# A 3x3 convolution in two transformed directions: patches of 4 rows x 2 columns for images 1 to 3, with their input sums in the order of the work

## The chip, the cores and the metric

One core of a Trainium2 chip runs the whole kernel. Its engines work side by side, each through its own queue in program order: PE multiplies matrices (with a path for loading weights, PEld), DVE (VectorE) and ACT (ScalarE) read and write SBUF and PSUM, POOL (GpSimd) works on SBUF, and SP issues DMAs. [...] The metric is the device time of the program in microseconds.

## What is computed

The input is x, four images of 256 channels, 48 x 48 pixels, f32. Two layers with a residual each:

- Layer 0: group norm of x, a 3x3 convolution 256 to 256 channels, batch norm with given statistics, relu; then q, k and v by a 256 to 768 product, attention over the 2304 pixels in 8 heads of 32, and a projection; the result is added to x.
- Layer 1: group norm; a 3x3 convolution to 45 channels gives, after a softmax over groups of nine, the weights of five dynamic 3x3 filters with dilations 1, 6, 12, 24 and 36; the input and the five filtered copies go through a 1x1 product (1536 to 256), then a batch norm over all images; the result is added.

The change concerns the 3x3 convolution of layer 0:

```
x = lax.conv_general_dilated(Vx, conv_w, window_strides=(1, 1), padding='SAME', ...)
x = x + conv_b[None, :, None, None]
inv = bn_gamma * lax.rsqrt(bn_var + BN_EPS)
x = x * inv[None, :, None, None] + (bn_beta - bn_mean * inv)[None, :, None, None]
x = jax.nn.relu(x)
```

## The kernel before

Channels lie on the 128 partitions in two halves (NH = 2). The loop over images (from `u_next = None` near L1792 on) has three kinds of stages. Image 0 first gets its convolution and q, k, v alone. Then, for each image b, comes its attention (`attention`, L978), which fills PE, DVE and ACT; and after it a mixed stage: the dynamic filters of image b (`dynamic_filters`, L1139) together with the convolution and q, k, v of image b + 1 (`conv_qkv`, L913). The last mixed stage, b = 3, has no convolution.

**The convolution.** `conv` (L765) works on patches of 4 output rows. An input of six rows is turned into six sums v[0] to v[5] (`inputs`, L773), each product i of the six multiplies its sum by its own transformed weights u[i], and `outputs` (L821) turns the six products back into four rows. Only the row direction is transformed: each product still runs over the three columns kx of the kernel. The image is split into two halves g of six patches each, so one matmul has 6 x 48 = 288 columns; a product has 2 g x 2 output groups o x 2 input halves h x 3 kx = 24 matmuls, an image 144. One PSUM buffer takes six matmuls (one product, g, o), and there are two such buffers (`ps_c`, L1797). The products come in `ORDER` = 1, 2, 3, 4, 0, 5. For image 0 DVE makes the input sums; for images 1 to 3 POOL does, on 600 elements at a time, all of them at the beginning of the convolution (`when`, L868 on). DVE and ACT empty PSUM: products 1 and 3 are copied by ACT, 2 and 4 become a sum and a difference with them on DVE, and 0 and 5 finish the rows, which ACT then scales, shifts and rectifies into `hid`.

**The weights.** `Made` (L728) makes u[i] from the convolution weights during image 0 and stores each to DRAM as `u_d[i]` (768 KB). For images 1 to 3 `taken` (L722) fetches them again, one product ahead, into a pool of two buffers; the same pool lends the attention its scratch and the last stage four homes.

**The order of the work.** The program is written out by hand (`manual_schedule`). A small planner, `Clock` (L687), holds a time for PE, DVE, ACT and POOL, advanced by a price per operation. In a mixed stage `drive` (L1625) holds several streams (weights' loads, far filters, near filters, the softmax of the filter weights, the 1x1 mix), each of which says from when it could go on; the first that is due by PE's time goes on, and if none is, one step of `other`, the convolution, is emitted; if that is used up, PE's time jumps. The near filter works in taps: ACT copies a weight row into PSUM (wb, L1448), DVE multiplies (prod, L1461), POOL adds (near, L1466). Before `drive`, the stage emits some convolution by `run(2400)` and `run(2500)` (L1653, L1667), between the steps of the group norm. What no stream left room for is emitted after it (`run(1e9)`), followed by q, k and v.

Fetches of u, of filter weights (ws) and stores stand in one queue, SP's. The two padded images (`pads`) alternate: one holds the image whose filters run, the other the normalized input of the convolution; both are loaded again from x at the start of an attention (`load_pad`, L1950).

Of the kernel before, what the change touches and what calls it, by code (L numbers as in the profile page):

```python
# [16 lines left out]
N = HH * WW  # L17
# [40 lines left out]
def conv_preact_kernel(  # L58
# [483 lines left out]
    u_d = tc.dram_tile([6, P, NH, 3, C], F32, name="u_d")  # L542
# [3 lines left out]
    with tc.tile_pool(name="w", bufs=1) as wpool, tc.tile_pool(  # L546
        name="act", bufs=1
    ) as act, tc.tile_pool(name="u", bufs=2) as upool, tc.manual_schedule():
# [12 lines left out]
        wqkv = wpool.tile([P, NH, 3, C], F32, tag="wqkv", name="wqkv")  # L561
        wp = wpool.tile([P, NH, C], F32, tag="wp", name="wp")
# [53 lines left out]
        bn_s6 = wpool.tile([P, NH], F32, tag="bn_s6", name="bn_s6")  # L616


        pads = []
        for j in range(2):  # L620
            t = act.tile([P, NH, PADW * PADW], F32, tag=f"pad{j}", name=f"pad{j}")
            t = t.rearrange("p h (r w) -> p h r w", w=PADW)
            nc.gpsimd.memset(t[:, :, 0, :], 0.0)
            nc.gpsimd.memset(t[:, :, PADW - 1, :], 0.0)
            nc.gpsimd.memset(t[:, :, 1 : PADW - 1, 0], 0.0)
            nc.gpsimd.memset(t[:, :, 1 : PADW - 1, PADW - 1], 0.0)
            pads.append(t)

# [58 lines left out]
        class Clock:  # L687
# [11 lines left out]
            def level(self):  # L699
                self.t = dict.fromkeys(self.t, max(self.t.values()))  # L700
# [21 lines left out]
        def taken(i):  # L722

            u = upool.tile([P, NH, 3, C], F32, tag="u", name=f"u_{i}")
            nc.sync.dma_start(out=u, in_=u_d[i])
            return u

        class Made:  # L728


            def __init__(self, wc, pool):
                self.w = [wc[:, :, 3 * j : 3 * j + 3, :] for j in range(3)]
                self.u = {}
                self.pool = pool

# [9 lines left out]

            def home(self, i):
                return upool.tile([P, NH, 3, C], F32, tag="u", name=f"u_{i}")
# [4 lines left out]
            def __call__(self, i):  # L752
# [9 lines left out]
                nc.sync.dma_start(out=u_d[i], in_=u[i])  # L762
                return u[i]

        def conv(b, gn, psum_tile, weights, ready, pool, hid, between):  # L765
# [115 lines left out]
            for at, i in enumerate(ORDER):  # L881
                u = ahead
                for g in range(2):
# [5 lines left out]
                    if g == 0 and at + 1 < len(ORDER):  # L889
                        ahead = weights(ORDER[at + 1])  # L890
                    for o in range(NH):
# [20 lines left out]

        def conv_qkv(b, gn, psum_tile, weights, ready, pool, between=()):  # L913

            hid = keep("h", f"hid_{b}")
            yield from conv(b, gn, psum_tile, weights, ready, pool, hid, between)
# [6 lines left out]
            for c in range(NCK):  # L923
                cols = slice(c * CH, (c + 1) * CH)
                for g in range(NH):
                    for s, dst, bias in ((0, q, Q_B), (1, k_, K_B)):
# [18 lines left out]
                        )  # L945
                        yield 2 * MM
# [31 lines left out]
        def attention(b, q, k_, vT, pools, spare, project, scratch):  # L978
# [132 lines left out]
            weigh(*steps[-1], prev)  # L1111
            close(last)
            return ao, chunk
# [25 lines left out]
        def dynamic_filters(b, ao, chunk, norm, other, pools):  # L1139
# [153 lines left out]
            def far():  # L1293

                for c in range(NCK):
# [6 lines left out]
                    held[0] = True  # L1302
                    for h in range(NH):
                        at = moved(
# [6 lines left out]
                        )  # L1311
# [313 lines left out]
            def drive(streams):  # L1625

                due = [next(s, None) for s in streams]
                while any(d is not None for d in due):
# [9 lines left out]
                    else:  # L1638
                        got = next(other, None)
                        if got is not None:  # L1640
                            spent[0] += got
                        elif soonest < NEVER:
                            clock.t["PE"] = soonest

            if alone:
                other = late()


            while chunk < NCK:
# [23 lines left out]
            if alone:  # L1673
                streams = [last_back(), *streams, last_loads()]
            drive(streams)
# [116 lines left out]
        u_next = None  # L1792
        norms = {}
        for b in range(B + 1):

            with tc.tile_pool(name=f"work1_{b}", bufs=2) as work1, tc.tile_pool(
# [13 lines left out]
                if b < B:  # L1810
                    weights, between = taken, ()
                    if b == 0:
# [62 lines left out]
                if b == 0:  # L1875
                    for j, _ in enumerate(other):
                        if j == 0:
# [5 lines left out]
                            nc.vector.tensor_scalar(bn_s6, bn_s, -1.0 / 6.0, None, ALU.mult)  # L1883
                            table(AF.Exp)
# [8 lines left out]
                else:  # L1893
                    if b == B:
# [15 lines left out]
                        for j in range(2):  # L1910
                            t = upool.tile([P, NH, 3, C], F32, tag="u", name=f"yu_{j}")
                            t = t.rearrange("p h k c -> p (h k c)")
# [150 lines left out]
```

## Time and profile before

| | |
|---|---|
| runs of the program | 2769.19, 2769.86, 2770.11 us; median 2769.86 |
| the profiled execution | 2766.55 us |
| its span, first to last instruction | 2764.8 us |
| PE, DVE, ACT, POOL busy | 2638.8, 2025.3, 1761.1, 632.3 us |
| mean granted PE clock | 0.99 |
| convolution and q, k, v of image 0 | to about 147 us |
| mixed stages | about 516 to 818, 1190 to 1492, 1861 to 2136 us |
| last stage | from about 2510 us |

Lines of the profile begin with the line of the program, the engine and the operation, then output <- inputs, the shape (partitions x elements) and xcount; after the bars come busy us and the mean of one in ns, then the idle time just before, with what ended it. In lines of the order of work the first number is the start in us and the second the length, and square brackets hold the idle time before it. In tables by stage each engine has its busy us and number of records; the last three columns are PE's clock, the share of the DMA engines, and GB/s. An f32 matmul leaves two records, and its own length is longer than the step to the next, since matmuls overlap.

### The profile page before, as it was taken

The page shows a single profiled execution, that of the slowest core. Times are in us where ns is not written, and L with a number is a line of the kernel's source. Part 1 is how long each engine was busy: PE and PEld are TensorE (multiplying, and loading weights), DVE is VectorE, ACT ScalarE, POOL GpSimd, SP SyncE. Part 2 cuts the span into 40 slices and gives each one's busy share as a digit, 9 for nine tenths or more (in the row PEclk, how much of TensorE's full clock was granted, in tenths as well). Part 3 has the DMA queues.
Part 4 walks back from the last instruction along what each step waited for, and adds up shares of the span by engine and source line. Part 5 has one row for each costly group of instructions (what it writes and reads, how often), then busy time and mean ns, then how long its engine had stood idle before and what let it go on. Part 6 is the DMA issues. An engine that isn't in the chain of part 4 may idle for free. (4 is left out here: it accounts for less than half of the span.)

```text
span 2764.8 us, 42248 instructions
## 1 busy us (share of the span) xinstructions
PE 2638.8 (95%) x17108; PEld 1135.8 (41%) x17108; DVE 2025.3 (73%) x1956; ACT 1761.1 (64%) x2153; POOL 632.3 (23%) x583
## 2 busy tenths in 40 slices
PE   7999999899999999989999999999999999999994
PEld 5632223455662222345565222245566222234452
DVE  6578888656539888856644988894664988885476
ACT  3488988633349888843336889882335988873244
POOL 5100100435400100054430001006542001000352
PEclk9999999999999999999999999999999999999997
DMA  5604544223422444423360345442335244432465
GB/s 216 156 24 103 109 98 104 58 77 90 104 56 58 101 102 97 109 57 75 84 132 9 81 98 112 101 87 56 93 92 150 55 96 95 101 87 68 118 181 182
DMA packets 132522, 267.35 MB, mean 97 GB/s; under 512 B 55656, under 2 KB 97552, under 8 KB 131424
## 3 DMA queue, kind: packets, MB, share of 16 engines
q0 software_dynamic: 25952, 135.74, 21.6%
q1 hardware_dynamic: 106368, 128.84, 17.7%
q8 instruction: 136, 2.23, 0.3%
q14 instruction: 66, 0.54, 0.1%
HBM read 107.40 MB, written 34.46 MB: 51 GB/s over the span
## 5 line engine op out<-in xcount | busy, mean ns | idle before, releaser
L1050 DVE TENSOR_TENSOR acc<-acc,p 128x2048 f32<-128x2048 f32 (+1 forms) x572 | 1061.1, 1855 | 115.6 <-ACT p L1014 64.9
L1014 ACT ACTIVATE p<-se 128x1536 f32<-128x1536 f32 x648 | 938.7, 1449 | 0.1
L1005 PE MATMUL so<-q,k 32*128 32x512 f32 (+1 forms) x1440 | 726.4, 592 | 13.5 <-ACT p L1013 12.7
L1005 PE MATMUL se<-q,k 32*128 32x512 f32 (+1 forms) x4320 | 735.1, 592 | 0.0
L1034 PE MATMUL num<-p,vT 128*32 128x512 f32 (+1 forms) x5760 | 705.1, 560 | 4.6 <-ACT p L1014 2.4
L1013 ACT ACTIVATE p<-so 128x512 f32<-128x512 f32 x648 | 388.4, 599 | 186.8 <-PE se L1005 80.0
L1466 POOL TENSOR_TENSOR near<-near,prod 128x768 f32<-128x768 f32 x192 | 348.8, 1817 | 431.4 <-DVE prod L1461 424.7
L1005 PEld LDWEIGHTS so<-q,k 32*128 32x128 f32 x1440 | 216.1, 183 | 529.0 <-ACT p L1013 489.8
L1034 PEld LDWEIGHTS num<-p,vT 128*32 128x32 f32 x5760 | 133.8, 108 | 478.8 <-issue 444.3
L1054 POOL DMA_DIRECT2D scratch<-p x124 | 105.5, 851 | 772.3 <-ACT p L1014 519.8
L1461 DVE TENSOR_TENSOR prod<-wb,pad 128x768 f32<-128x768 f32 x192 | 181.9, 953 | 87.6 <-ACT wb L1448 75.6
L1561 PE MATMUL py<-far,wsc 128*128 128x384 f32 x704 | 236.7, 488 | 0.0
L1005 PEld LDWEIGHTS se<-q,k 32*128 32x128 f32 x4320 | 226.7, 183 | 5.4 <-ACT p L1014 4.1
L1448 ACT COPY wb<-ws 128x384 f32<-128x384 f32 x216 | 108.7, 507 | 171.3 <-DVE prod L1461 137.6
L1170 ACT COPY far<-far 128x512 f32<-128x512 f32 x82 | 87.9, 1099 | 137.4 <-PE far L1395 134.6
L1052 POOL DMA_DIRECT2D scratch<-p x32 | 17.9, 559 | 669.7 <-ACT p L1014 508.3
L1561 PEld LDWEIGHTS py<-far,wsc 128*128 128x128 f32 x704 | 131.1, 190 | 87.3 <-issue 1.8
L897 PE MATMUL pc<-cv_q,u 128*128 128x288 f32 x576 | 151.8, 415 | 8.2 <-DVE cv_q L788 6.2
L1197 PE MATMUL pg<-pad,wcat 128*45 128x384 f32 x864 | 149.1, 493 | 10.0 <-ACT lg L1255 4.4
L897 PE MATMUL pc<-cv_k,u 128*128 128x288 f32 x576 | 153.3, 410 | 4.3 <-DVE yt L832 2.7
L930 PE MATMUL pq<-hid,wqkv 128*128 128x384 f32 x384 | 125.6, 487 | 1.7 <-DVE yt L832 0.6
L897 PEld LDWEIGHTS pc<-cv_q,u 128*128 128x128 f32 x576 | 108.7, 192 | 43.2 <-DVE cv_q L788 6.3
(252 smaller groups left out, 2368.3 us busy)
## 6 DMA issues: line engine op xcount, KB each, us to landing
scratch<-p POOLq DMA_DIRECT2D x156, 768.0 KB, 5.7
ws<-w_d SPq DMA_DIRECT2D x216, 192.0 KB
pad<-in_x SPq DMA_DIRECT2D x14, 1152.0 KB
u<-u_d SPq DMA_DIRECT2D x18, 768.0 KB
xst<-in_x POOLq DMA_DIRECT2D x36, 192.0 KB, 6.9
x_d<-pad SPq DMA_DIRECT2D x36, 192.0 KB
y_d<-y SPq DMA_DIRECT2D x14, 384.0 KB
u_d<-u SPq DMA_DIRECT2D x6, 768.0 KB
```

Of the source, the lines that this page charges most:

```text
L897: nc.tensor.matmul(m, u[:, h, kx, o * P : (o + 1) * P], halves[g][:, h, i, :, kx : kx + WW], start=(h == 0 and kx == 0), stop=(h == NH - 1 ...
L930: nc.tensor.matmul(pq[:, :CH], wqkv[:, i, s, g * P : (g + 1) * P], hid[:, i, cols], start=(i == 0), stop=(i == NH - 1),)
L1005: nc.tensor.matmul(dst[:, at : at + n], k_[r, g, m * P : (m + 1) * P], q[r, g, q0 : q0 + n], start=True, stop=True,)
L1013: nc.scalar.activation(p[:, 0, :], s1, AF.Exp, scale=QS)
L1014: nc.scalar.activation(p[:, 1:, :], s3, AF.Exp, scale=QS)
L1034: nc.tensor.matmul(st["num"][r, at : at + n], vT[:, m, g * P + j * D : g * P + (j + 1) * D], p[:, j, at : at + n], start=(m == 0 and not s ...
L1050: nc.vector.tensor_tensor(st["acc"][:, js], other[:, js], p[:, js], ALU.add)
L1197: nc.tensor.matmul(pg[64 * s : 64 * s + NG, :CH], wcat[:, ii, k, :], shifted(ii, cc, k // 3 - 1, k % 3 - 1), start=(i == 0 and k == 0), st ...
L1448: nc.scalar.copy(pw[:, :CH], fetched[c, k][0])
L1461: nc.vector.tensor_tensor(prod.rearrange("p h (r w) -> p h r w", w=WW), wb, src, ALU.mult)
L1466: nc.gpsimd.tensor_tensor(cat, cat, prod, ALU.add)
L1561: nc.tensor.matmul(py[c][:, o, :CH], wsc[:, n * NH + i, o * P : (o + 1) * P], rhs, start=(n == 0 and i == 0), stop=(n == order[-1] and i = ...
```

## The change

For images 1 to 3 the column direction is transformed too. A patch is now 4 rows x 2 columns: from each row sum v[i], four column sums (j = 0 to 3) are made from columns two apart, and each product (i, j) is one plain 256 x 256 product with its own weights. The whole image's 12 x 24 patches fill one matmul of 288 columns, so a tile (i, o) has 4 j x 2 h = 8 matmuls, an image 12 tiles and 96 matmuls. A PSUM buffer takes two matmuls. Image 0 keeps the old form.

- `Blocks` holds the input sums. `stage0` (two ACT scalings and four POOL sums of 1200 elements, with the column sums of product 1 among them) is emitted at the end of the attention before, through `following[0]()` ahead of `close(last)`; with it goes the fetch of the second tile's weights. `scaled` and the column sums of product 2 follow with the first tile. `rest` is a stream of its own, first in `drive`: the other row sums, then the column sums of 3, 4, 0 and 5, the last three each once an earlier product has passed, since they are written over `pads`. Column sums of products 1 to 3 go to POOL, of the others to POOL or DVE by the planner's times (`either`).
- `conv_blocks` multiplies and empties: per tile, j = 1 is copied by ACT; with j = 2 a sum and a difference are made; j = 0 and j = 3 give the two columns of each patch, written two elements apart. Where the planner finds DVE more than 500 ns behind, ACT copies from PSUM first and the sum goes to DVE or POOL. The row direction is then undone on 576 elements at a time (`before`, `after`), and a relu is emitted only once its input is due.
- `need` tells `drive` from when the convolution could go on; until then the planner's PE time is not given to it.
- `Made.convert` turns the stored weights of a product from three kx to four j during image 0: per output group two ACT scalings, three DVE sums and a store of 512 KB, staged in `pads[1]`. It is called one product late, in the second half of each product, and at the end. `u_d` holds 12 pieces of 512 KB.
- `ring`, 3 x 1024 elements, takes the place of the pool of two; it holds three tiles' weights, fetched two tiles ahead.
- Pads are cleared again at each attention. The planner's `level` leaves POOL out, POOL's time is set to 12.5 us after PE's at the start of a mixed stage, and `own` takes the later of its two copies.

The core of the diff:

```
-    u_d = tc.dram_tile([6, P, NH, 3, C], F32, name="u_d")
+    u_d = tc.dram_tile([6, NH, P, NH * 4 * P], F32, name="u_d")
...
+        ring = wpool.tile([P, 3 * 1024], F32, tag="ring", name="ring")
...
+            def convert(self):
+                i = self.ready.pop(0)
+                four = pads[1].rearrange("p h r w -> p (h r w)")
+                at = NH * 4 * C * (self.made % 2)
+                self.made += 1
+                for o in range(NH):
...
+                    nc.scalar.mul(f[:, :, 0], of[:, :, 0], 2.0)
+                    nc.scalar.mul(f[:, :, 3], of[:, :, 2], 2.0)
+                    tt = nc.vector.tensor_tensor
+                    tt(f[:, :, 1], of[:, :, 0], of[:, :, 2], ALU.add)
+                    tt(f[:, :, 2], f[:, :, 1], of[:, :, 1], ALU.subtract)
+                    tt(f[:, :, 1], f[:, :, 1], of[:, :, 1], ALU.add)
+                    nc.sync.dma_start(out=u_d[i, o], in_=t)
...
+                    if g and at:
+                        weights.convert()
...
+            def stage0(self):
+                v, d = self.v, self.d
+                nc.scalar.mul(v[0], d[2], 4.0)
+                nc.scalar.mul(v[5], d[1], 4.0)
+                self.sum(v[0], d[4], v[0], ALU.subtract)
+                self.sum(v[5], d[3], v[5], ALU.subtract)
+                self.sum(v[1], v[0], v[5], ALU.add)
+                self.along(1)
+                self.sum(v[2], v[0], v[5], ALU.subtract)
...
+            def along(self, i, js=(1, 2, 0, 3)):
+                z = self.of[i].rearrange("p (j h n) -> p j h n", j=4, h=NH)
+                d = [self.v[i][:, :, :, t : t + WW - 1 : 2] for t in range(4)]
+                for j in js:
+                    x, y = ((0, 2), (1, 2), (2, 1), (1, 3))[j]
+                    op = ALU.add if j == 1 else ALU.subtract
+                    to = z[:, j].rearrange("p h (t s) -> p h t s", s=XT)
+                    if i in ORDER[:3]:
+                        nc.gpsimd.tensor_tensor(to, d[x], d[y], op)
+                        self.end[i, j] = clock("POOL", 1400)
+                    else:
+                        self.end[i, j] = either(to, d[x], d[y], op)
...
+            for t, (i, o) in enumerate(TILES):
+                u = us.pop(t)
+                y = target(i, o).rearrange("p (n s) -> p n s", s=2)
+                for n, j in enumerate((1, 2, 0, 3)):
...
+                    for h in range(NH):
+                        nc.tensor.matmul(
+                            m, u[:, h, j], z[:, h], start=(h == 0), stop=(h == NH - 1)
+                        )
...
+                                if t + 2 < len(TILES):
+                                    us[t + 2] = taken(t + 2)
+                                if t == 0:
+                                    blocks.along(ORDER[1])
+                                before(i, o)
...
+                    if n == 0:
+                        one = pool.tile([P, XN], F32, tag="one", name=f"one_{b}_{i}_{o}")
+                        nc.scalar.copy(one, m)
...
+                        else:
+                            tt(two[:, 0], m, one, ALU.add)
+                            tt(two[:, 1], one, m, ALU.subtract)
...
+                            if j == 0:
+                                tt(to, m, two[:, 0], ALU.add)
+                            else:
+                                tt(to, two[:, 1], m, ALU.subtract)
...
+                        if n == 3:
+                            after(i, o, y.rearrange("p n s -> p (n s)"))
...
-                        got = next(other, None)
-                        if got is not None:
-                            spent[0] += got
-                        elif soonest < NEVER:
-                            clock.t["PE"] = soonest
+                        open_at = need[0]()
+                        if open_at <= clock.t["PE"]:
+                            got = next(other, None)
...
+            clock.level()
+            if not alone:
+                clock.t["POOL"] = clock.t["PE"] + 12500
...
+                streams.insert(0, coming[-1].rest() if coming else iter(()))
...
             weigh(*steps[-1], prev)
+            following[0]()
             close(last)
+            following[1]()
```

## The prediction

> **What bounds the kernel now.** I read the page's busy shares first, then a table by stage of the stretch after image 0's attention (511 to 818 us), then the order of work inside it. The page says:
>
> ```profile
> PE 2638.8 (95%) x17108; PEld 1135.8 (41%) x17108; DVE 2025.3 (73%) x1956; ACT 1761.1 (64%) x2153; POOL 632.3 (23%) x583
> L897 PE MATMUL pc<-cv_q,u 128*128 128x288 f32 x576 | 151.8, 415 | 8.2 <-DVE cv_q L788 6.2 <-POOL cv_q L788 2.0
> ```
>
> PE is busy for 95% of the span, with no stage far below. The second line, a group with its shape, is half of the convolution: each f32 matmul leaves two records, so 576 are 288 matmuls. The stages after attention 0, columns PE, PEld, DVE, ACT, POOL:
>
> ```profile
> 522.00:546.00 24.00, 20.82 (x87) 11.82 (x88) 8.94 (x13) 9.13 (x16) 23.24 (x18) 0.89 0.18 50
> 546.00:745.00 199.00, 196.26 (x896) 114.94 (x895) 119.21 (x163) 63.83 (x109) 100.06 (x58) 1.00 0.32 80
> 745.00:771.00 26.00, 26.00 (x108) 20.22 (x107) 11.66 (x28) 9.24 (x17) 0.00 (x0) 1.00 0.88 182
> ```
>
> The 199 us are the dynamic filters of image 0 with image 1's convolution as filler: PE full, DVE 60%, POOL 50%, ACT 32%. The next 26 us are convolution alone, the rest that found no gap. In the order of PE's work:
>
> ```profile
> 747.44 5.98 PE L897 MATMUL pc<-cv_q,u 128*128 128x288 f32 x24
> 753.26 5.98 PE L897 MATMUL pc<-cv_k,u 128*128 128x288 f32 x24
> ...
> 770.72 31.12 PE L930 MATMUL pq<-hid,wqkv 128*128 128x384 f32 x96
> ```
>
> Twelve matmuls start 5.82 us before the next twelve: 0.485 us each, back to back. 108 of image 1's 288 records stand here, so 54 of its 144 matmuls; 90 were filler.
>
> [...] In image 3's convolution, beside filters on POOL, VectorE's order of work has
>
> ```profile
> 2060.31 1.08 DVE L827 SCALAR_TENSOR_TENSOR yt<-cs 128x288 f32<-128x288 f32 x1
> 2061.43 1.95 DVE L856 TENSOR_TENSOR cs<-cs 128x288 f32<-128x288 f32 x1
> 2063.48 0.46 DVE L832 TENSOR_TENSOR yt<-pc,cs 128x288 f32<-128x288 f32 x1
> ```
>
> 0.46 us is the free price of the first two; with a PSUM input (the third) it stays 0.46. [...]
>
> **The change, part by part.** *Matmuls removed.* Images 1 to 3 go from 6 products x 2 halves x 2 output groups x 6 = 144 matmuls of 288 columns to 6 x 2 x 4 x 2 = 96 of 288. 48 x 0.485 = 23.3 us of PE an image, 69.8 in all. PE is the limit where they stand, so this is the gross gain.
>
> *Input sums.* Row sums: 12 of 1200 elements take the place of 24 of 600 (1.45 us, rows L788 to L796), about equal, 34 us. New are 24 column sums of 576 elements, at 1.4 us 34 us: 12 always on POOL, 12 on POOL or VectorE. POOL in the 199 us goes from 100 to about 129 us, 65%.
>
> *Outputs.* Per tile (12 an image) VectorE takes two sums of 288 from PSUM and two more into strided columns: 4 x 0.45 = 1.8, 21.6 an image. On 576 elements (0.75 us, the nearest row being L1757's 576-element sum at 752 ns) come 8 sums after products 2 and 4, 4 after 0 and 5, and 8 before them: 15 us. With half of the late column sums, 4.5, that is 41 us against 19.7 before (16 x 0.45 + 8 x 0.46 + 8 x 0.46 + 8 x 0.64). Some goes to ACT (32% busy) where the plan finds VectorE late. About 30 more fall into the 199 us, DVE 119 to 149, and some 20 two-SBUF operations there meet POOL at 65%: at about 0.6 us each (the 0.6 to 1.5 seen above, times that share) 12 us. DVE then stands near 80%: no bound by its sum, but late often.
>
> *The start of a stage.* POOL's first sums are moved ahead of the attention's last close. ACT is free of exponentials at 515.1; two scalings of 1200 (1.1 each) end at 517.5, three POOL sums (2.8) at about 526, the first column sum at 527.5, the others each 1.4 later. VectorE's last 2.29 us acc sum and POOL can block one another once: +2. The first convolution matmul began at 527.94 before; now it starts near 528 and is fed one group in 1.4 us. Queued behind on PE is the norm's pm matmul (531.44), and behind that the normalizing and the first filter matmul (537.54). VectorE also takes group two's sums (0.9) ahead of the norm's aggregate, and with two PSUM buffers the third group of the second tile waits for ACT's 2.3 us normalizing. I take +2.0 a stage (0 to 5). POOL's three memsets (1.5) and the moved v2 sum come later, with nobody waiting before 543.
>
> *Groups of two matmuls.* A PSUM buffer is filled in 0.97 us, not 2.9; with two buffers the drain of group n must be over within about one group. Group two's drain is 0.9 plus a semaphore, just not enough. Image 3's stretch at 2046 to 2087 us, DVE 73% busy, is the nearest row: 1.83 + 0.84 us of PE idle for VectorE over 12 groups, 0.22 a group. 48 groups make 10.7; where filter matmuls are at hand they fill it, so I take two thirds, 7 us an image (0 if all is filled, 24 if each group stalls 0.5).
>
> *The end.* Before, only the last half's relu stood between convolution and q/k: no gap at 770.72. Now the last tile needs PE to VectorE 0.5, a sum of 0.75, relu 0.67, with semaphores 2.5 us in which PE has nothing if the filters are done. +2.5 an image (0 if they aren't).
>
> *Transfers.* u is fetched in 12 pieces of 512 KB, lead two tiles (16 x 0.485 = 7.8 us in plain convolution), against six of 768 KB with 11.6. They stand in SP's queue behind ws fetches, which waited up to 9.3 us for a wb copy; in the mixed stretch a tile lasts longer than that, so nothing. The four pad loads (748.07 to 769.81) now wait for the convolution's last read, since products 4, 0 and 5 use the pads; the 47 us of q, k and v cover them. Uncovered, they would delay the attention's normalizing by up to 22 us. Clearing a pad on POOL at the attention's start lies beside an idle POOL.
>
> *Image 3.* Its filters run on to 2110.2 on POOL (last near sum), then late stores, while PE ends its stage near 2136; saving over 23 there meets the filter chain. I add 2 for that and late u pieces.
>
> *Image 0.* Six conversions of 4 ACT scalings (about 0.4) and 6 VectorE sums of 256 (about 0.42), 2.5 us a batch, against 2.9 us groups with VectorE at 51.5 of 75 us: +2 (0 to 6), the last one standing ahead of q/k. The clock levels, `at = max` and the ring's layout: nothing.
>
> **Sum.** Images 1, 2: -23.3 + 2.0 + 7 + 2.5 = -11.8 each; image 3 -9.8; image 0 +2: -31.4. The profiled execution took 2766.55 (span 2764.8 and 1.75 around it), so 2735.2; the runs' median stands 3.3 above it: **2738**.
>
> **Rivals.** *Nearly the whole gain.* Before's 90 filler matmuls can be nearly all the new convolution; if gaps and relu vanish beside filters, only start (-21.3 x 3) and conversion remain: -62, 2708. For it: PE idled only 2.7 of 199 us. Against: POOL had no second stream then.
>
> *The filters stretch and eat it.* The near chain goes ACT wb, VectorE prod, POOL near, 48 taps an image; POOL waited 93.7 us for prod and ACT 44.6 for its release in this stage. 0.4 us more a tap is 19 us, which PE cannot fill once the convolution is used up; net about -2 to -4 an image with half the start hidden: 2762. For it: all three engines get more work. Against: the taps pause anyway.
>
> *Slower, by VectorE in front of PSUM.* A two-SBUF sum locked out by POOL stands ahead of group two's drain, PE waits in order, and the filter matmuls queue behind the waiting one. Break-even is (23.3 - 2 - 2.5) / 48 = 0.39 us a group; at 0.7, three times before's 0.22, an image costs 14.8 more than before: 2770 + 44 + 2 = 2816, at 0.55 2794. For it: 1.95 us for 0.46 above, more locked operations, a third of the slack. Against: the scalar engine is offered the copies, and filters part the groups.
>
> **How the numbers follow.** A measurement of this kernel can tell about 0.2%, 5.5 us, from no change. Forecast (saving 12 to 50) 0.51; nearly whole gain 0.16; eaten by the filters 0.13, of which half still faster by 5.5; slower 0.20. Faster 0.51 + 0.16 + 0.07 = 0.74, same 0.06, slower 0.20. The range goes from 2700 (gross gain 69.8) to 2794 (0.55 us a group); the forecast alone would be 2720 to 2758.
>
> **What would show it.** Right: 192 records of pc for images 1 to 3 each; the stretch with filters still near 200 us with hardly any plain convolution after it; PE idle for VectorE before pc of 5 to 10 us an image; q/k starting 9 to 14 us sooner after the attention than the 254 us of before (516.5 to 770.7). Wrong: a stretch well over 215 us with PE idle for near or far (filters), idle on "two" or y over 19 us an image (slower), column sums on POOL above 2 us, PE waiting for u, or image 0's 147 us growing by more than 6.

## The result, and the profile after

The changed kernel takes 2770.1 us (median of 12 runs, 2765.2 to 2780.9), the kernel before 2769.78 in the same session: ratio 1.0007, 95% interval 0.9995 to 1.0018. The forecast was 2738. PE works through a third fewer matmuls in the convolutions of images 1 to 3, and the program is no faster.

The page of the changed kernel begins its busy shares with:

```profile
PE 2596.0 (94%) x16820; PEld 1089.6 (39%) x16820; DVE 2142.2 (77%) x2045; ACT 1796.7 (65%) x2242; POOL 741.7 (27%) x641
```

PE is busy 42.8 us less than before (2638.8), DVE 116.9 more, POOL 109.4 more. Where the time went is seen by stages. Measured from the first projection matmul of a mixed stage to the first attention matmul after it, in the profiled executions (2766.55 us before, 2768.08 after):

| us | image 0 | attentions 0 to 3, sum | mixed 0 | mixed 1 | mixed 2 | last |
|---|---|---|---|---|---|---|
| before | 147.9 | 1503.3 | 295.1 | 295.3 | 269.0 | 254.1 |
| after | 152.1 | 1509.5 | 290.9 | 292.1 | 265.2 | 256.6 |
| difference | +4.2 | +6.2 | -4.2 | -3.2 | -3.8 | +2.5 |

The mixed stages keep 11.2 of the 69.8 us that the removed matmuls are worth, and the rest of the program gives those back. The first mixed stage by windows (columns PE, PEld, DVE, ACT, POOL, then PE's clock, DMA share, GB/s), split at the same kind of places as before:

```profile
528.00:552.00 24.00, 20.26 (x86) 10.97 (x86) 10.02 (x20) 6.60 (x11) 23.80 (x16) 0.93 0.22 61
552.00:775.00 223.00, 207.82 (x917) 120.46 (x915) 168.12 (x203) 87.37 (x158) 128.46 (x74) 0.98 0.29 79
775.00:819.00 44.00, 44.00 (x162) 30.48 (x162) 13.13 (x26) 17.72 (x31) 0.61 (x4) 1.00 0.67 128
```

The stretch with filters was 199 us long with 2.7 us of PE idle; it is 223 us long with 15.2 idle. POOL's 128.5 us is what was forecast (129), in a longer stretch; DVE has 168, where 149 and 12 of waiting were forecast. The order of PE's work at its end:

```profile
751.24 1.24 PE L1139 MATMUL pc<-pad,ring 128*128 128x288 f32 x4 [0.27 <-ACT two L1159]
754.01 2.85 PE L1854 MATMUL py<-near,wsc 128*128 128x384 f32 x8 [1.53 <-POOL near L1759]
756.69 1.45 PE L1219 MATMUL pq<-hid,wqkv 128*128 128x384 f32 x4
...
774.90 2.85 PE L1854 MATMUL py<-near,wsc 128*128 128x384 f32 x8
777.59 25.96 PE L1219 MATMUL pq<-hid,wqkv 128*128 128x384 f32 x80
```

The convolution is used up at 752.5, 224 us into the stage; the last filter matmuls (py) end at 777.7, 249.5 us into it, against 222.4 before. In between q and k are the filler. So the plain convolution after the filters, 26 us before, is gone, as forecast, but the filters are 27 us later. The second mixed stage is like the first. In the third the filters end at 199.3 us, before the convolution (206.1).

Over the whole mixed stage PE is busy 272.2 us and idle 18.7; before it was 289.5 and 5.6. So PE's work fell by 17.3, not 23.3, and its idle time grew by 13.1. The waits of PE in it, the longest first (in all, times, longest):

```profile
PE far L1688 <- DVE amat L1660: 6.1, 1, 6.1
PE pc L1139 <- ACT one L1154: 2.9, 1, 2.9
...
PE xa L1608 <- DVE own L1464: 2.4, 1, 2.4
```

And what stood in front of the longest of them, in the order of DVE's, POOL's and PE's work:

```profile
578.87 3.03 POOL L981 TENSOR_TENSOR cv_q<-pad,cv_q 128x1200 f32<-128x1200 f32 x1
579.56 2.95 DVE L1068 TENSOR_TENSOR cv_v<-cv_q,cv_v 128x576 f32<-128x576 f32 x1
581.86 3.22 POOL L981 TENSOR_TENSOR cv_q<-cv_q,cv_v 128x1200 f32<-128x1200 f32 x1
582.44 2.96 DVE L1068 TENSOR_TENSOR two<-one,two 128x288 f32<-128x288 f32 x1
585.32 1.00 DVE L1660 COPY_PREDICATED amat<-along_y,bmat 128x768 f32<-128x768 uint32 x1
586.37 2.08 PE L1688 MATMUL far<-amat,xT 64*128 64x256 f32 x8 [6.10 <-DVE amat L1660]
```

DVE's two sums of the new convolution (L1068, two SBUF inputs) cost 0.76 and 0.45 us where they are free. Here each takes almost 3 us and ends 0.3 to 0.6 us after POOL's 1200-element sum beside it. No semaphore is waited for in this time: the trace shows the DVE instruction as running. So DVE waits here for POOL in a second way, beside the semaphores: 2.95 us for a sum that takes 0.76. The far filter's copy is queued behind them on DVE, and PE, in order, waits for that copy.

The sums of `either` on DVE as groups (count, then busy us and mean ns):

```profile
L1068 DVE TENSOR_TENSOR two<-one,two 128x288 f32<-128x288 f32 x9 | 11.1, 1239 | 0.1
L1068 DVE TENSOR_TENSOR pad<-cv_q 128x576 f32<-128x576 f32 x7 | 9.4, 1380 | 0.0
```

In all, 22 of 288 elements and 20 of 576 take 49.7 us in this stage. At the free prices they would take 22 x 0.452 + 20 x 0.757 = 25.1: 24.6 us of DVE's time is waiting that the trace books as busy.

### The profile page after: what moved, and what is told of

Same layout as the page of the kernel before. It is cut to its first block, busy times and chain, and to the rows that moved or that the text cites. A ratio compares the mean times of both kernels' runs of the same rounds, so it can differ in the third digit from the quotient of the medians.

```text
span 2766.3 us, 42026 instructions
## 1 busy us (share of the span) xinstructions
PE 2596.0 (94%) x16820; PEld 1089.6 (39%) x16820; DVE 2142.2 (77%) x2045; ACT 1796.7 (65%) x2242; POOL 741.7 (27%) x641
## 5 line engine op out<-in xcount | busy, mean ns | idle before, releaser
L1344 POOL DMA_DIRECT2D ring<-p x124 | 105.5, 851 | 779.8 <-ACT p L1304 464.8
L1462 ACT COPY far<-far 128x512 f32<-128x512 f32 x92 | 97.4, 1105 | 143.4 <-PE far L1688 142.0
L1342 POOL DMA_DIRECT2D ring<-p x32 | 17.9, 558 | 640.8 <-ACT p L1304 481.5
L1688 PE MATMUL far<-amat,xT 64*128 64x256 f32 x576 | 86.0, 416 | 18.3 <-DVE amat L1660 18.3
L1219 PEld LDWEIGHTS pq<-hid,wqkv 128*128 128x128 f32 x384 | 73.6, 194 | 60.6 <-ACT hid L1089 7.0
L1340 DVE TENSOR_TENSOR acc<-p,p 128x2048 f32<-128x2048 f32 x36 | 82.3, 2285 | 19.6 <-ACT p L1304 19.6
```

The lines of the kernel that those rows point to most:

```text
L1219: nc.tensor.matmul(pq[:, :CH], wqkv[:, i, s, g * P : (g + 1) * P], hid[:, i, cols], start=(i == 0), stop=(i == NH - 1),)
L1340: nc.vector.tensor_tensor(st["acc"][:, js], other[:, js], p[:, js], ALU.add)
L1344: nc.gpsimd.dma_start(out=extra, in_=p[:, 1:], accum_op=ALU.add)
```

## The experiments

Two theories, and smaller ones. *Lock*: the mixed stages are long because POOL's sums block DVE's sums on SBUF. *Load*: they are long because POOL and DVE have more to do. Beside these, image 0's conversion and the planner's edits.

The stages in the last column are of one profiled execution each, and these differ: in the rows "large POOL sums in two", "no undoing of rows", "no conversion arithmetic" and "zeros on POOL" it took 6 to 8 us more than the median, in "outputs from PSUM only" 6 us less.

| edit of the changed kernel | median us | ratio to before, 95% | mixed stages of the profiled execution |
|---|---|---|---|
| none | 2770.1 | 1.0007, 0.9995 to 1.0018 | 290.9, 292.1, 265.2 |
| outputs from PSUM only | 2780.6 | 1.0036, 1.0024 to 1.0048 | 295.1, 291.9, 270.4 |
| large POOL sums in two | 2762.8 | 0.9970, 0.9959 to 0.9981 | 290.8, 291.9, 263.7 |
| small sums on POOL only | 2805.5 | 1.0123, 1.0106 to 1.0140 | 292.5, 296.5, 296.0 |
| no undoing of rows | 2747.9 | 0.9911, 0.9893 to 0.9929 | 284.4, 282.7, 270.0 |
| no conversion arithmetic | 2769.9 | 0.9998, 0.9990 to 1.0005 | 292.7, 291.9, 277.1 |
| no later input sums | 2758.2 | 0.9957, 0.9940 to 0.9973 | 288.2, 285.2, 267.3 |
| (before) planner's edits alone | 2770.0 | 1.0002, 0.9993 to 1.0011 | 295.0, 295.3, 269.1 |
| PSUM only, small sums on POOL | 2764.8 | 0.9978, 0.9967 to 0.9990 | 286.7, 290.4, 266.7 |
| no undoing, no later sums | 2734.1 | 0.9872, 0.9857 to 0.9887 | 279.7, 278.7, 256.8 |
| fills on POOL | 2727.3 | 0.9848, 0.9833 to 0.9863 | 279.2, 278.9, 248.7 |
| the two first gains together | 2762.0 | 0.9974, 0.9965 to 0.9983 | 286.3, 286.8, 270.9 |
| zeros on POOL | 2762.4 | 0.9968, 0.9957 to 0.9980 | 288.6, 290.4, 264.3 |
| fills on POOL, longer | 2727.5 | 0.9847, 0.9830 to 0.9863 | 280.2, 278.6, 251.5 |
| all POOL sums cut | 2783.5 | 1.0054, 1.0037 to 1.0071 | 295.8, 295.8, 270.1 |
| all cut, PSUM only, small on POOL | 2756.4 | 0.9952, 0.9942 to 0.9962 | 284.4, 289.1, 263.2 |

### Image 0 and the planner

The conversion's arithmetic left out, its stores kept (what is stored is then a constant, with which POOL fills the buffer once, a line not shown):

```
-                    nc.scalar.mul(f[:, :, 0], of[:, :, 0], 2.0)
-                    nc.scalar.mul(f[:, :, 3], of[:, :, 2], 2.0)
-                    tt(f[:, :, 1], of[:, :, 0], of[:, :, 2], ALU.add)
-                    tt(f[:, :, 2], f[:, :, 1], of[:, :, 1], ALU.subtract)
-                    tt(f[:, :, 1], f[:, :, 1], of[:, :, 1], ALU.add)
```

> Changed kernel without the arithmetic of the weights' conversion in image 0 (ACT scalings and VectorE sums left out, the stores kept, so the weights are not the right ones). Image 0's stage grew by 4.2 us in the profile; if the conversion's arithmetic did that, 2765 to 2767 and the first attention starts near 148 us; if the stores did, no change.

And the planner's edits alone, on the kernel before (`level` without POOL, `own` with the later of its copies):

```
-                self.t = dict.fromkeys(self.t, max(self.t.values()))
+                at = max(t for engine, t in self.t.items() if engine != "POOL")
+                self.t = {engine: max(at, t if engine == "POOL" else 0.0) for engine, t in self.t.items()}
...
-                        at = moved(
+                        at = max(at, moved(
```

> Kernel before, with only the two small planner changes (levels leave POOL out; own takes the later of two copies). The last stage grew by 2.4 us in the profile, where nothing else changed: if these did it, 2771 to 2774; if it was chance, 2768 to 2771.

Neither moves the time: 2769.9 and 2770.0. Leaving out the arithmetic of the conversion gains nothing, and image 0 is not shorter without it (154.7 us in the profiled execution, where POOL's fill is extra); the planner's edits don't lengthen the last stage or the attentions. No change is what was expected if the stores lengthen image 0, but that was not tested by itself; what lengthens the attentions is open too. The last stage's +2.5 is no more than executions differ by: with the same instructions it took 254.2 us without the conversion's arithmetic and 260.1 in a kernel below (zeros on POOL), at granted clocks of 0.93 and 0.90.

### Less work for DVE and POOL

The row direction is not undone (and column outputs come from PSUM):

```
-                    either(s, y, blocks.first[o], ALU.add)
-                    either(d, blocks.first[o], y, ALU.subtract)
...
-                    either(s12, s12, s34, ALU.subtract)
...
-                    axpy(d12, d34, -8.0, d12)
```

> Changed kernel with outputs from PSUM only, and without the undoing of the row direction (20 operations of 576 elements an image left out, so the result is another). VectorE's convolution work is then about that of before, with hardly a two-SBUF operation. Lock and load: most of the 23.3 us an image comes through, 2715 to 2735. Sums, or the order of emission by itself: 2755 to 2772.

The input sums after product 1 left out, with ACT's scalings for them (the removed body of `rest` is not shown):

```
-                    {2: hid[:, :z], 3: hid[:, z:], 4: self.pad[0], 0: self.pad[1], 5: self.pad[0]}
+                    {i: self.pad[0] for i in (2, 3, 4, 0, 5)}
...
+                if i != 1:
+                    self.end.update(((i, j), 0.0) for j in js)
+                    return
```

> Changed kernel without input sums after those of product 1 and the row sum of product 2 (products 2, 3, 4, 0 and 5 read the pad as it is, so the result is another). POOL loses some 55 us a mixed stage, VectorE about 9. Lock: VectorE meets only near adds, 8 to 12 us a stage, 2735 to 2748. Sums: the same or more. Load: only the 9 us of VectorE, 2760 to 2768.

Both:

> Both reductions at once: the row-direction undoing of the outputs is left out (20 operations of 576 an image), the input sums after product 1 are left out (later products read the first pad), and column outputs always come from PSUM on VectorE; the output is not the reference's. PE's work is that of the changed kernel. Alone they gave 2747.9 and 2758.2 against 2770. Load or lock (the stretch is as long as VectorE's and POOL's work and their collisions make it, and nothing else holds it): the two add up or more, 2715 to 2732, the mixed stages near 275 to 280 us. Order (the start of a stage, the groups of two matmuls and the clock keep the rest): less than the sum of the two, 2738 to 2746.

Measured 2747.9, 2758.2 and 2734.1. The first and the second fell between the bands, the third too, but their gains, by the ratios against 1.0007, nearly add up: 26.6 + 13.9 = 40.5 us against 37.4 together. So over half of the lost 70 us goes with this work on DVE and POOL. The runs take the work away together with its collisions, so they don't say which of the two costs.

### Lock or load

POOL only writes: each of its sums becomes two fills of the same output, which read no SBUF.

```
-                nc.gpsimd.tensor_tensor(out, x, y, op)
+                nc.gpsimd.memset(out, 0.01)
+                nc.gpsimd.memset(out, 0.01)
```

> In the changed kernel each POOL sum of the convolution of images 1 to 3 is replaced by two fills of its output with a constant, which read no SBUF and should take POOL about as long; the sums are left out, so the output is not the reference's. VectorE's, ACT's and PE's work is as in the changed kernel. Lock (VectorE's two-SBUF operations are blocked while POOL reads SBUF): the either-sums on VectorE fall from about 1.3 us (576) and 1.07 (288) to about 0.76 and 0.45, the 6.1 us wait before far goes, and the time is 2750 to 2763. Load (POOL's time counts, whatever it does): 2767 to 2774, with the sums on VectorE as long as before. Should the fills be much shorter than the sums, the trace shows it and the run says less.

2727.3, a gain beyond the band. But a pair of fills of 1200 elements took 2.2 us, less than the sum (2.73 free, 2.98 on average here), and constant data might have helped PE (though the changed kernel, with real data, has a granted clock of 1.00 too from 150 to 180 us into the stage, where PE is busy all 30.0 us). Two further runs take these doubts apart, one with a third, half-sized fill:

```
+                nc.gpsimd.memset(out[:, 0], 0.01)
```

> The run with fills on POOL, with a third fill of half the size after each pair of 1200 elements, so that POOL takes about 2.78 us for it, the free price of the sum that it stands for (2.73); the sums are left out, so the output is not the reference's. Lock (what counts is that POOL reads SBUF while VectorE wants to): nearly as before the lengthening, 2727 to 2740. Load (POOL's time): most of the gain of the fills goes, 2755 to 2770. Half and half: 2740 to 2755.

and one in which POOL writes a constant too, but reads two operands for it:

```
-                nc.gpsimd.tensor_tensor(out, x, y, op)
+                nc.gpsimd.tensor_tensor(out, y, y, ALU.subtract)
```

> A control for the run with fills on POOL (2727 us): in the changed kernel POOL's sums of the convolution of images 1 to 3 become differences of one operand with itself, so that they write a constant, zero, but still read SBUF twice and take as long; the sums are left out, so the output is not the reference's. If constant data in the convolution made the difference (a higher clock for TensorE): 2725 to 2745. If it is that POOL reads SBUF, or the time that it takes: 2764 to 2774, with the sums of VectorE on two SBUF inputs as long as in the changed kernel (50 us in the first mixed stage).

The longer fills give 2727.5, the same as the shorter ones and in the lock theory's band; the zeros give 2762.4. In the first mixed stage POOL is busy 144.6 us with the longer fills and 144.3 with the zeros: the same time, constant data in both, DVE's and ACT's work and the order of emission untouched, and 34.9 us between them, 11.6 an image. What differs is that POOL reads SBUF. A fill also has no input to wait for, but POOL's waits hardly differ: 12.2 us before the first fill and 12.3 before the first sum with zeros, 71.0 and 73.7 in all before the near sums. The zeros fell 1.6 us below their band and are 7.7 us faster than the changed kernel. They are no exact copy of its load: the difference of an operand with itself takes 2.19 us for 1200 elements where free, not 2.73, and POOL is busy 144.3 us, not 152.6. The groups of `either` with zeros, and then with the longer fills:

```profile
L1068 DVE TENSOR_TENSOR two<-one,two 128x288 f32<-128x288 f32 x9 | 10.5, 1163 | 0.1
L1068 DVE TENSOR_TENSOR pad<-cv_q 128x576 f32<-128x576 f32 x7 | 8.9, 1300 | 0.0
```

```profile
L1072 DVE TENSOR_TENSOR two<-one,two 128x288 f32<-128x288 f32 x9 | 7.1, 789 | 0.5 <-ACT two L1163 0.4
L1072 DVE TENSOR_TENSOR pad<-cv_q 128x576 f32<-128x576 f32 x7 | 7.3, 1081 | 0.0
```

All 42 of them take 45.5 us with zeros, 35.5 with fills. The place of the jam, with fills, in the order of POOL's and DVE's work (some short rows in between are left out):

```profile
574.01 1.11 POOL L981 MEMSET cv_q<- 128x1200 f32 x1
574.13 0.44 DVE L1072 TENSOR_TENSOR two<-one,two 128x288 f32<-128x288 f32 x1
575.17 1.10 POOL L982 MEMSET cv_q<- 128x1200 f32 x1
575.59 0.76 DVE L1072 TENSOR_TENSOR cv_v<-cv_v,cv_q 128x576 f32<-128x576 f32 x1
576.33 0.60 POOL L983 MEMSET cv_q<- 128x600 f32 x1
576.38 0.76 DVE L1072 TENSOR_TENSOR cv_v<-cv_q,cv_v 128x576 f32<-128x576 f32 x1
```

DVE runs at its free prices, 0.44 and 0.76, right beside POOL. So in these traces DVE's sum of 576 elements on two SBUF inputs takes 2.95 us beside a POOL sum, which reads SBUF, and 0.76 beside a fill, which only writes it. What is left over the free price with fills, 35.5 - 25.1 = 10.4 us, is put down to the near filter's sums, the only ones left on POOL there that read SBUF (48 of 1.84 us); that is the author's estimate and was not tested by itself.

One run doesn't fit a simple reading. Without the later input sums POOL has even less to do in the first mixed stage (122.8 us) than with the longer fills, and the filters end sooner (233.6 us against 238.8), and yet the program takes 2758.2 us. Its plan is another one, since the planner's times for POOL change: more of the convolution is left when the filters are done, and PE then waits for the last relus, 2.3, 2.3 and 6.7 us in the three stages (with the longer fills only in the third, 2.9). Whether that is all that it loses was not tested; the 34.9 us hold for the changed kernel's order of work.

The window 568 to 588 us shows what the jam does to PE, first in the changed kernel, then with the longer fills:

```profile
568.00:588.00 20.00, 13.12 (x66) 9.60 (x64) 17.65 (x20) 5.51 (x13) 12.78 (x6) 0.88 0.32 94
```

```profile
568.00:588.00 20.00, 17.52 (x95) 11.68 (x95) 11.58 (x23) 9.89 (x20) 10.31 (x15) 1.00 0.40 107
```

PE is idle 6.9 us in the changed kernel and 2.5 with the longer fills, and the granted clock is 0.88 and 1.00. The loss is thus more than the wait: over the whole stage, with zeros against longer fills, idle time is 15.3 against 10.3 us, and busy time, for the same matmuls, 273.3 against 269.9 at a mean clock of 0.97 against 0.99.

### Shorter POOL instructions

The 1200-element sums as two of 600:

```
+                for h in range(NH):
+                    nc.gpsimd.tensor_tensor(out[:, h], x[:, h], y[:, h], op)
```

> Changed kernel, each row sum of 1200 elements on POOL as two of 600: the same work, half the length of a hold. Lock: VectorE's waits of up to 3 us become at most 1.5, 3 to 5 us a mixed stage, 2755 to 2762. Load and sums: within 3 us of the changed kernel, 2768 to 2774.

Nearly all of POOL's sums cut, the 1200 into four, the column sums of products 1 to 3 and the near filter's sums into two (those that `either` gives to POOL, 14 in the first mixed stage, stay whole):

```
+                for h in range(NH):
+                    for t in range(2):
+                        nc.gpsimd.tensor_tensor(
+                            out[:, h, t * TJ : t * TJ + TJ], x[:, h, t * TJ : t * TJ + TJ],
+                            y[:, h, t * TJ : t * TJ + TJ], op,
+                        )
...
-                    nc.gpsimd.tensor_tensor(cat, cat, prod, ALU.add)
+                    for h in range(NH):
+                        nc.gpsimd.tensor_tensor(cat[:, h], cat[:, h], prod[:, h], ALU.add)
```

> In the changed kernel each POOL sum is cut into shorter instructions of the same work: those of 1200 elements into four, column sums of 576 and the filters' near sums of 768 into two. Lock: a VectorE operation waits for a shorter instruction, 2750 to 2762 (the 1200-element sums alone, in two, gave 2762.8). Load: the same or longer by POOL's overhead of some 100 further instructions an image, 2768 to 2785.

In two: 2762.8, 0.3% faster than before and 0.8 us above the lock theory's band. The wait before far is 3.6 us instead of 6.1:

```profile
PE far L1689 <- DVE amat L1661: 3.6, 1, 3.6
```

All cut: 2783.5, a clear miss of the lock theory's band, and inside the load theory's. The order of work shows two things. In one place DVE gets in between the pieces:

```profile
585.09 4.42 POOL L983 TENSOR_TENSOR cv_q<-cv_q,pad 128x300 f32<-128x300 f32 x4
586.49 1.14 DVE L1074 TENSOR_TENSOR cv_v<-cv_v,cv_q 128x576 f32<-128x576 f32 x1
587.66 1.21 DVE L1074 TENSOR_TENSOR cv_v<-cv_q,cv_v 128x576 f32<-128x576 f32 x1
```

In another, earlier in the stage, it does not:

```profile
557.35 9.37 DVE L1074 TENSOR_TENSOR cv_q<-cv_q,two 128x288 f32<-128x288 f32 x1 [1.70 <-ACT cv_q L1176]
558.23 3.14 POOL L983 TENSOR_TENSOR cv_k<-cv_k,cv_v 128x300 f32<-128x300 f32 x4
561.33 5.08 POOL L1063 TENSOR_TENSOR hid<-cv_k 128x288 f32<-128x288 f32 x8
567.60 2.26 PE L1145 MATMUL pc<-hid,ring 128*128 128x288 f32 x4 [7.84 <-DVE two L1171]
```

One sum of 288 elements, 0.45 us where free, waits through these twelve pieces and the end of those before, which stand back to back, and ends 0.3 us after the last. In the changed kernel the same sum took 1.28 us. DVE's sums from PSUM are queued behind it, and PE waits 7.8 us for them, its longest wait in the stage; in the other two stages the same sum takes 7.7 us and PE waits 6.2. The forecast, and the lock theory's band, had a block last for one instruction; here it lasts for a run of them. Why DVE gets its turn in one place and not in the other stays open.

So the 42 sums take 49.2 us together, against 49.7 uncut, but not for the same reason: without the long one the others take 39.8. Over the three stages PE waits 20.2 us behind the long sum, while its waits for amat fall from 18.3 to 8.1; the stages are 13.4 us longer in all. POOL loses too: the four pieces of 300 take 4.42 us in the first place, and over the stage its sums for the convolution went from 68.8 to 78.0 us and the near filter's from 88.1 to 97.5. How much of the loss that longer time makes was not tested by itself.

### Where the outputs are summed

Column outputs always from PSUM on DVE. Such a sum has one SBUF input; in the changed kernel's mixed stages none of the 53 took more than 0.46 us, whatever POOL did:

```
             def busy_dve():
-                return clock.t["DVE"] > max(clock.t["ACT"], clock.t["PE"]) + 500
+                return False
```

> Changed kernel, but VectorE always takes its column outputs from PSUM (ACT never copies them to SBUF first). Theory lock (a VectorE operation with two SBUF inputs waits for POOL's running sum, and the filters' steps wait behind it): some 20 operations an image lose their lock, VectorE is freed of some 13 us a mixed stage, the filters end 4 to 8 us earlier: 2748 to 2760. Theory load (VectorE simply has too much work, locked or not): as many VectorE operations as before, 2767 to 2775. Theory sums (POOL's input sums hold up the near adds): no change, 2767 to 2773.

All sums of `either` on POOL:

```
-            if clock.t["POOL"] + 1400 * part <= clock.t["DVE"] + 1000 * part:
+            if True:
```

> Changed kernel, every sum that may go to VectorE or POOL goes to POOL. Lock and load: VectorE loses about 50 us a mixed stage, 2738 to 2758. Sums: POOL gains some 40 us a stage and the near adds come later, 2780 to 2800.

Both edits:

> Changed kernel, column outputs from PSUM on VectorE, all sums that may go to either on POOL: VectorE keeps only operations with a PSUM input and six axpy of two SBUF inputs an image. Lock: the least lock of all, below e1 and e3, 2735 to 2752. Sums: POOL has some 25 us more, 2775 to 2790.

2780.6, 2805.5, 2764.8. The first was outside every band: PE now waits 6.2 us for `two` in the first mixed stage and 9.5 in the third, since DVE's sums stand in front of PE's next group and the 14 other sums of `either` still get locked (23.3 us in the first stage, 10.6 at the free price). The second was above every band. POOL, busy 198.8 of 292 us in the first mixed stage, is the limit in the third, 296.0 instead of 265.2 us, where PE waits 28.1 us for POOL's column sums. Together they fell between the bands and are better than the changed kernel. What the traces show of it: DVE then has no sum of the convolution on two SBUF inputs but its scaled ones (`axpy`), while POOL is spared the 30 sums of 288 that came from the copied outputs (22 were DVE's and 8 POOL's).

Last, the gains together, first with the large sums in two, then with all POOL sums cut:

> The two changes that made the changed kernel faster together, with the whole computation: column outputs always from PSUM on VectorE, every other small sum on POOL, and POOL's 1200-element sums as two of 600. Alone: 2764.8 and 2762.8 against 2770. If both take away the same collisions of VectorE with POOL: 2760 to 2766. If they add up: 2754 to 2760. If POOL, now with more instructions, becomes late: 2766 to 2775.

> The same cuts, with column outputs always from PSUM on VectorE and every other small sum on POOL (with the 1200-element sums alone cut, this gave 2762). Lock: 2745 to 2760. If POOL, which has every small sum and more instructions, becomes late: 2765 to 2785.

2762.0 (0.9974): not the sum of the two gains, as would be if both remove the same collisions. With all cut 2756.4, in the lock theory's band, ratio 0.9952 (0.9942 to 0.9962): the best kernel with the whole computation, 13.3 us faster than before. Its waits in the first mixed stage:

```profile
PE pc L1145 <- ACT one L1160: 4.3, 2, 2.9
PE pc L1145 <- DVE two L1171: 3.7, 3, 2.7
PE pq L1225 <- ACT hid L1095: 2.3, 1, 2.3
```

No wait for amat is among the larger ones now. The filters end 226.9 us into the stage, 8 us ahead of the convolution, and the wait for the last relu (`hid`) appears. In the third stage PE waits 11.8 us for `two`.

## Why the prediction was wrong

The step that failed is in the part on outputs: "some 20 two-SBUF operations there meet POOL at 65%: at about 0.6 us each ... 12 us. DVE then stands near 80%: no bound by its sum, but late often." The mechanism was named; its size and its consequence were wrong.

- *Size.* There were 42 such sums, not 20: where the plan finds DVE late, ACT copies an output from PSUM to SBUF, and the sum, at most 0.46 us from PSUM, becomes one with two SBUF inputs. They waited 24.6 us in all in the first mixed stage. The convolution's work on DVE came to about 62 us (49.7, with 4.5 of `axpy` and 8 from PSUM) against 41 + 12.
- *Consequence.* The forecast charged nothing for "late often". DVE's queue holds the far filter's copies and the near filter's products as well, so a late sum delays the filters. The rival "the filters stretch and eat it" had this: it put the net at -2 to -4 an image, and the stages gave -4.2, -3.2 and -3.8; it put the stretch at 19 us, and it was 27; and its sign, a stretch over 215 us with PE idle for far, came true. That the net fits so well is in part luck: its cause was given as more work per tap on three engines. The lock with the convolution's sums on POOL is about half of the loss: of the 69.8 us that the program fails to gain, 34.9 come back when POOL fills instead of reading for the same time. In the three mixed stages of the profiled executions it is 33.0 (843.3 us with zeros, 810.3 with fills) of the 58.6 by which they fall short of the gross gain (69.8 - 11.2). Of the stretch itself it is the smaller part: the last filter matmul ends 247.2 us into the stage with zeros and 238.8 with fills, 8.4 of 27. The rest of the stretch goes with the work on DVE and POOL: without undoing and later sums that matmul ends at 223.7, near the 222.4 of before. The lock costs PE idle time there (15.3 us with zeros, 10.3 with fills) and clock (0.97 and 0.99), while much of the stretch is filled with q and k.
- *The gross gain*, 23.3 us an image: 192 records of pc an image stand in the trace, as worked out. PE's busy time fell by 17.3. With the longer fills it is 269.9, so 2.3 of the missing 6 us go with the idle time and the clock. Most of the other 3.7 stand in the convolution's matmuls themselves: PE is busy with pc for 75.1 us of the stage before and for 55.0 with the longer fills, 0.52 and 0.57 us a matmul where 0.485 had been read from matmuls back to back. So 20.1 us go, not 23.3. That the smaller groups, parted by filters, make a matmul longer is likely but was not tested.
- *Groups of two matmuls*, +7: not seen. Waits of PE for a drain of group two or of y are 0.5 us in the stage, with ACT given most of the copies. In the whole computations with the outputs kept on DVE, the waits for `two` came to 3.7 to 6.2 us in the first stage and 9.5 to 13.3 in the third: the term was of about the right size for a plan that the changed kernel doesn't follow.
- *The end*, +2.5: not paid for images 1 and 2, since the filters end after the convolution, and its "0 if they aren't" holds. For image 3 they end first, and PE waits 5.4 us for the last relus, more than forecast. In the last kernel above it is 2.3 in each stage ("pq <- hid"). Of the parts of the 2.5, the 0.5 from PE to DVE and what the semaphores take were the author's estimate; the relu of 576 elements takes 0.87, not 0.67.
- *The start*, +2.0: in the first stage the first filter matmul comes 16.9 us after the first projection matmul, 15.3 before: +1.6. Its mechanism, the copy behind ACT's 2.3 us normalizing, shows as the 2.9 us wait for `one`. The block that it names, POOL's first sum behind DVE's last acc sum, came true: 4.46 us instead of 2.73, beside an acc sum of 2.29.
- *POOL*: 129 forecast, 128.5 measured. The column sums were put at the price of contiguous ones, 1.4 us, as the author's estimate; they take 1.16 us where free and 1.38 on average with their waits.
- *Image 0*: +2 (0 to 6) forecast, +4.2 measured, but not by the arithmetic, which can be left out without gain. *Attentions and last stage*: nothing forecast, +6.2 and +2.5 measured; the second is within what executions differ by, and for the first nothing tried here shows why.
- *The rival on the slow side*, PE standing before PSUM for locked sums, was not what happened; with outputs from PSUM only, it is in part, and the ratio is 1.0036 instead of 1.0007.

## What to carry to other kernels

A sum moved to POOL was not free for DVE: DVE's operations with two SBUF inputs that met it waited, the longest to its end (2.95 us for 0.76), and the trace books the wait as busy time. Count DVE's operations with two SBUF inputs and POOL's that read SBUF in the same stretch, take the length of POOL's instruction as the price of a meeting at worst (2.95 us here), or of a whole run of instructions where they stand back to back (9.4 us here), and look at what is queued behind on DVE. Copying an output from PSUM to SBUF to relieve DVE turned sums that were not locked out here (at most 0.46 us) into ones that were (1.24 us on average for nine of them).

## What the runs showed of the hardware

- Fills of 1200 elements on POOL took 1.10 us and left DVE's two-input sums beside them at 0.44 and 0.76 us; a sum of 1200 made them wait up to its end, 2.95 us.
- DVE's sums with one input in PSUM took at most 0.46 us in the same stages.
- Cutting POOL's sums shortened most of DVE's waits (2.95 to about 1.2 us), but one sum of 288 elements a stage took 9.4, 7.7 and 7.7 us, through a run of pieces back to back, and the total over 42 sums stayed (49.7 to 49.2 us).
- On POOL the difference of an operand with itself took 2.19 us for 1200 elements, the sum of two operands 2.73.
- PE lost more than its idle time: over the 20 us with 6.9 us idle the granted clock was 0.88, and over the same place with 2.5 us idle 1.00.
- POOL's column sums, reading every second f32 (576 elements in 1.16 us), cost no more per element than its contiguous sums (1200 in 2.73 us): 2.0 against 2.3 ns.
